# A linear recurrence beside a feed-forward layer: the first batch's preparation cut into pieces between the feed-forward steps, and three small operations moved to other engines

## The chip, the cores and the metric

The kernel runs on one core of one Trainium2 chip. The metric is the device time of one execution in microseconds (us). The engines are named as in the profile: PE is TensorE (matrix products), PEld its weight loads, DVE is VectorE, ACT is ScalarE, POOL is GpSimd, SP is SyncE, which only issues DMAs here.

## The reference, cut to what matters

The reference runs four pairs of layers over x (4 batches of 512 tokens, 512 wide); every pair adds a gated cross-attention and a gated feed-forward result to x. The change touches two of these eight parts. One is the feed-forward part of pair 0, with sign weights:

```python
hidden = jnp.einsum('bsd,hd->bsh', x, sign(up_weight)) * up_scale     # 512 -> 2048
out = jnp.einsum('bsh,dh->bsd', relu(hidden), sign(down_weight)) * down_scale
```

The other is the "cross-attention" of pair 2, which is a state-space recurrence over the context. It depends on the context alone, not on x, so the kernel may compute it early:

```python
x = jnp.einsum('ed,bld->bel', in_proj_w, ctx)             # 512 channels e, 512 positions l
xc = conv_of_4_taps(x, conv_w)                            # along l, each channel by itself
u = silu(xc + conv_b)
x_dbl = jnp.einsum('ke,bel->bkl', x_proj_w, u)            # dt_lo, B (16 rows), C (16 rows)
delta = softplus(dt_proj_w @ dt_lo + dt_proj_b)
state = state * exp(delta * A[:, n]) + (delta * u) * B[n] # for each of 16 n, along l
y = sum_n state_n * C[n] + D * u
```

The last step, the gate with silu of the layer norm of x, comes later in the kernel and is not touched.

## The kernel before, in words

The program is built with a tile framework that orders each engine's queue itself: it takes what its own estimate holds ready, by priority. Where a product on PE is "tied" to the one before it, PE's order is the order in which the program was written. All products of this stage except the transposes of the layer norm are tied.

The stage in question is `s1` (feed-forward) with the generator `states()` (recurrence) running beside it. In the profile it lies between about 646 and 1441 us. `s1` makes 64 steps: `i` counts 8 halves of batches (256 tokens each), `f2` counts 8 pairs of hidden blocks. One step issues these, in this order:

1. the chain `s_ph` on PE (16 records of 128x256, line L244),
2. `aside(1)`: one `next` of the recurrence,
3. `behind.end()`: the chain `s_acc` of the step before (8 records of 128x512, L905),
4. the two Relu evictions `s_hT` on ACT (L936),
5. `aside(1)`: one more `next` of the recurrence.

`aside` runs its `next` with a priority 4000 places later, so that the recurrence fills what the feed-forward part leaves free; PE's order is as written all the same.

The recurrence has one slot for each batch b (4), channel block e (4) and pair of n (8): 128 slots, one `yield` each. A slot first issues `summed` for the slot before, which adds two states into PSUM with eight products by the identity (`s_y`, L268), then issues two states. A state costs these: broadcast rows `s_B` and `s_C` (256 KB DMAs on SP, L1154), the product `s_db` on DVE (L1156), `s_da`, an Exp, on ACT (L1157), the scan `s_h` on DVE (L1158), and the product of `s_h` with `s_C` on POOL (L1159). `s_h` has 7 buffers, so DVE may run at most 7 states ahead of PE. When a channel block ends, `channels_done` copies the sums out of PSUM on ACT (L1190 to L1192: two half copies into `r`, one copy into `r0`), and in the next slot `rest` makes y on DVE with two operations (L1195, L1198) and writes it out.

Each batch needs its preparation first. `pieces(b)` returns nine pieces: four times `channels(e)` (product `s_pi`, copy `s_xp` on ACT, four taps on DVE at L1097 and L1099, Silu into u), then `low` (product `s_pd`), `raw(0)`, `delta((0, 1))`, `raw(2)`, `delta((2, 3))` (product `s_pv`, then Abs, Relu, Exp and Ln on ACT, with five operations on DVE for each block, L1129 to L1137). The pieces write u, delta and delta times u to DRAM rows, and the states read them back. The PSUM tile of `s_pi`, `s_pd` and `s_pv` has one buffer, so each of these products waits until ACT has read the one before.

The pieces of batches 1 to 3 are dealt one by one into every third slot of the batch before, in its channel blocks e = 0 to 2. Those of batch 0 have no batch before. They are issued in one go by `next(states)` ahead of the 64 steps, at ordinary priority, so on PE they stand ahead of the first `s_ph`.

The 64 steps make 128 `next`, just the 128 slots. The last `summed` and `channels_done` come after them. The feed-forward weights (eight tiles of 1 MB) are loaded and put through Sign on ACT (L875, L884) at the start of the stage.

Of the kernel before, what the change touches and what calls it, by code (L numbers as in the profile page):

```python
# [16 lines left out]
ALU = mybir.AluOpType  # L17
# [4 lines left out]
S = 512  # L22
# [26 lines left out]
class Net:  # L49
# [816 lines left out]


    def s1(self, states, aside):
        nc, a = self.nc, self.a
        FC = 2048 // P  # L870
        wu = []
        for c in range(DC):
            t = self.w(f"s1_wu_{c}")
            nc.sync.dma_start(t, a["s1_upT"][c * P : (c + 1) * P, :])
            nc.scalar.activation(t, t, AF.Sign)  # L875
            wu.append(t)
        wd = []
        for c in range(4):
            t = self.w(f"s1_wd_{c}")
            v = t.rearrange("p (f n) -> p f n", f=4)  # L880
            nc.sync.dma_start(
                v, a["s1_downT"][c * 512 : (c + 1) * 512, :].rearrange("(f p) n -> p f n", p=P)
            )
            nc.scalar.activation(t, t, AF.Sign)  # L884
            wd.append(v)
        us = self.s("s1_us", FC)
        nc.sync.dma_start(us, a["s1_us"].rearrange("(f p) -> p f", p=P))
        ds = self.bcast("s1_ds", a["s1_ds"])
        osc = self.s("s1_os", 1)
        nc.sync.dma_start(osc, a["s1_os"].partition_broadcast(P))  # L890
        nc.vector.tensor_scalar(ds, ds, osc, None, op0=ALU.mult)

        behind = Behind()
        xTs = {0: self.lnT("s1_0", 0)}
        next(states)
        accs = {}
        HT = TB // 2

        def down(i, f2, hT):
            if f2 == 0:  # L900
                accs[i] = [self.mm(f"s1_acc_{i}_{t}") for t in range(HT)]
            for j in range(2):
                f = 2 * f2 + j
                for t in range(HT):
                    ins = nc.tensor.matmul(  # L905
                        accs[i][t],
                        lhsT=hT[:, j, t * P : (t + 1) * P],
                        rhs=wd[f // 4][:, f % 4, :],
                        start=(f == 0),
                        stop=(f == FC - 1),  # L910
                    ).ins
                    self.tie(ins)
            if f2 == FC // 2 - 1:
                for t in range(HT):
                    r = self.t(f"s1_r_{i}_{t}")
                    nc.vector.tensor_tensor(r, accs[i][t], ds, op=ALU.mult)
                    self.residual(i * HT + t, r, self.gf[:, 0:1])

        for i in range(2 * NB):
            b, cols = i // 2, slice(i % 2 * HT * P, (i % 2 + 1) * HT * P)  # L920
            for f2 in range(FC // 2):
                if i % 2 and f2 == 0 and b + 1 < NB:
                    xTs[b + 1] = self.lnT(f"s1_{b + 1}", b + 1)
                ph = self.mm(f"s1_ph_{i}_{f2}").rearrange("p (j n) -> p j n", j=2)
                for j in range(2):
                    fs = slice((2 * f2 + j) * P, (2 * f2 + j + 1) * P)
                    self.chain(
                        ph[:, j, :], [(wu[c][:, fs], xTs[b][:, c, cols]) for c in range(DC)],
                        tied=True,
                    )  # L930
                aside(1)
                behind.end()
                hT = self.t(f"s1_hT_{i}_{f2}").rearrange("p (j n) -> p j n", j=2)
                for j in range(2):
                    f = 2 * f2 + j
                    nc.scalar.activation(  # L936
                        hT[:, j, :], ph[:, j, :], AF.Relu, scale=us[:, f : f + 1]
                    )
                behind(down, i, f2, hT, more=True)
                aside(1)  # L940
        behind.end()
# [105 lines left out]
    def states(self):  # L1047

        nc, a = self.nc, self.a
# [12 lines left out]
        cw = fixed("s4_cw", [P, EC, 4])  # L1062
# [16 lines left out]
        def pieces(b):  # L1079
            part = lambda k, e: rows[b][k][e * P : (e + 1) * P, :]  # L1080
            room = {}

            def channels(e):
                if e == 0:
                    room["cx"] = self.context("s4", b)
                    room["u"] = self.up.tile([P, EC, S], F32, tag="u4", name=f"s4_u_{b}", bufs=1)
                pi = pre(f"pi_{b}_{e}")
                self.chain(
                    pi,
                    [(wi[:, c, e * P : (e + 1) * P], room["cx"][:, c, :]) for c in range(CC)],  # L1090
                    tied=True,
                )
                xp = self.tp.tile([P, S + 3], F32, tag="t", name=f"s4_xp_{b}_{e}")
                nc.gpsimd.memset(xp[:, 0:3], 0.0)
                nc.scalar.copy(xp[:, 3 : S + 3], pi)
                xc = self.t(f"s4_xc_{b}_{e}")
                nc.vector.tensor_scalar(xc, xp[:, 0:S], cw[:, e, 0:1], None, op0=ALU.mult)  # L1097
                for k in range(1, 4):
                    nc.vector.scalar_tensor_tensor(  # L1099
                        xc, xp[:, k : S + k], cw[:, e, k : k + 1], xc, op0=ALU.mult, op1=ALU.add  # L1100
                    )
                u = room["u"][:, e, :]
                nc.scalar.activation(u, xc, AF.Silu, bias=vec[:, 0, e : e + 1])
                nc.sync.dma_start(part("u", e), u)

            def low():
                pd = pre(f"pd_{b}")[0 : 3 * N]
                self.chain(pd, [(wx[:, e, :], room["u"][:, e, :]) for e in range(EC)], tied=True)
                room["low"] = self.t(f"s4_low_{b}")
                nc.scalar.copy(room["low"][0 : 3 * N], pd)  # L1110
                nc.sync.dma_start(rows[b]["bc"], room["low"][N : 3 * N])

            def raw(e):
                pv = pre(f"pv_{b}_{e}")
                self.chain(pv, [(wdt[:, e * P : (e + 1) * P], room["low"][0:N])], tied=True)
                bias = vec[:, 1, e : e + 1]
                room["v", e], room["z", e] = (self.t(f"s4_{k}_{b}_{e}") for k in ("v", "z"))
                nc.scalar.activation(room["z", e], pv, AF.Abs, bias=bias)
                nc.scalar.activation(room["v", e], pv, AF.Relu, bias=bias)

            def delta(es):


                raw(es[1])
                vs, zs = ([room.pop((k, e)) for e in es] for k in ("v", "z"))
                z1s = [self.t(f"s4_z1_{b}_{e}") for e in es]
                for z, z1 in zip(zs, z1s):
                    nc.scalar.activation(z, z, AF.Exp, scale=-1.0)
                    nc.vector.tensor_scalar(z1, z, 1.0, None, op0=ALU.add)  # L1129
                    nc.vector.scalar_tensor_tensor(z, z1, -1.0, z, op0=ALU.add, op1=ALU.subtract)  # L1130
                for z1 in z1s:
                    nc.scalar.activation(z1, z1, AF.Ln)
                for e, v, z, z1 in zip(es, vs, zs, z1s):
                    nc.vector.tensor_tensor(z1, z1, z, op=ALU.subtract)
                    nc.vector.tensor_tensor(v, v, z1, op=ALU.add)
                    nc.sync.dma_start(part("dl", e), v)
                    nc.vector.tensor_tensor(z1, v, room["u"][:, e, :], op=ALU.mult)  # L1137
                    nc.sync.dma_start(part("du", e), z1)

            return (  # L1140
                [lambda e=e: channels(e) for e in range(EC)]
                + [low]
                + [lambda: raw(0), lambda: delta((0, 1)), lambda: raw(2), lambda: delta((2, 3))]
            )

# [30 lines left out]
        yield  # L1176
        for piece in pieces(0):
            piece()
        yield
        def row(k, b, e):  # L1180
            t = self.qp.tile(
                [P, S], F32, tag=f"r{k}", name=f"s4_r{k}_{b}_{e}", bufs=1 + (k != "u")
# [4 lines left out]
        def channels_done(b, e, u, y):  # L1187

            r, r0 = self.t(f"s4_yr_{b}_{e}"), self.t(f"s4_y0_{b}_{e}")
            nc.scalar.copy(r[0:64], y[64:128, 1, :])  # L1190
            nc.scalar.copy(r[64:128], y[0:64, 1, :])
            nc.scalar.copy(r0, y[:, 0, :])  # L1192

            def rest():
                nc.vector.scalar_tensor_tensor(  # L1195
                    u, u, vec[:, 2, e : e + 1], r0, op0=ALU.mult, op1=ALU.add
                )
                nc.vector.tensor_tensor(u, u, r, op=ALU.add)  # L1198
                nc.sync.dma_start(rows[b]["y"][e * P : (e + 1) * P, :], u)

            return rest
# [984 lines left out]
```

## Time and profile before

| | us |
|---|---|
| median of 3 runs | 3196.8 (3187.31 to 3198.38) |
| the profiled execution | 3203.01 |
| its span | 3201.1 |
| PE busy in the span | 2821.5 (88%) |
| DVE busy in the span | 1952.0 (61%) |
| ACT busy | 1196.0 (37%) |
| POOL busy | 975.8 (30%) |
| the stage: its first product (`s_pi`) starts, the first product of the next stage (`s_pkv`) starts | 646.62 to 1440.69 |
| first and last scan of the stage | 695.48, 1427.41 |

The shares are means over eight parts with different limits, so the stage must be read by itself. The page's line engine operation groups give a busy total, a mean in ns of one instruction, and the idle time of the engine before it. A view by windows gives busy time by stretch. A timeline row gives start, duration, engine, line, operation and count.

### The profile page before, as it was taken

The numbers are of one execution on the slowest core, as the hardware profiler recorded it, in microseconds if no ns is written. First come the engines' busy times: TensorE is split into PE (matmuls) and PEld (weight loads), VectorE is DVE, ScalarE is ACT, GpSimd is POOL, SyncE is SP. The second block draws the span as 40 slices with busy tenths as digits, with TensorE's granted clock in tenths as the row PEclk, the third lists the DMA queues.
The fourth block names the chain that finished last, engine by engine and source line by source line (L and its number), as shares of the span: only waits on it lengthen the run. The fifth ranks groups of instructions, "written<-read, shape, count | busy, mean of one in ns | idle before, by whom it ended". The sixth has DMA issues, their size and how long they took to land.

```text
span 3201.1 us, 43082 instructions
## 1 busy us (share of the span) xinstructions
PE 2821.5 (88%) x15776; PEld 1442.0 (45%) x15776; DVE 1952.0 (61%) x3212; ACT 1196.0 (37%) x2061; POOL 975.8 (30%) x939
## 2 busy tenths in 40 slices
PE   6899898768988989997786699977999999989999
PEld 2333333234444444443344588862333333345774
DVE  6565666378897979987788311118666666735004
ACT  2343443365554445433222111112554545521331
POOL 3465654516555655760000122210000000001440
PEclk8899999879999989999897699997999999989999
DMA  4000000177676767862212599973000000013996
GB/s 133 7 1 7 1 1 1 20 252 238 195 229 176 236 206 224 250 196 84 77 64 90 176 320 326 322 259 137 14 29 14 29 1 1 1 53 122 379 384 225
DMA packets 266897, 438.75 MB, mean 137 GB/s; under 512 B 32400, under 2 KB 114576, under 8 KB 265152
## 3 DMA queue, kind: packets, MB, share of 16 engines
q1 hardware_dynamic: 250624, 386.72, 37.8%
q0 software_dynamic: 13760, 45.10, 3.9%
q10 hardware_dynamic: 2304, 4.20, 0.3%
q8 instruction: 126, 2.06, 0.3%
q14 instruction: 83, 0.68, 0.1%
HBM read 370.79 MB, written 65.13 MB: 136 GB/s over the span
## 4 chain that ended last, share of the span: by engine, by line
PE 60%; DVE 16%; POOL 9%; ACT 6%; issue 6%; DMA 3%; SPq 0%; DVEq 0%; POOLq 0%; ACTq 0%
PE s_pl L268 12%; PE s_po L244 11%; PE pg_s L244 7%; PE s_ph L244 6%; POOL s_h L1159 6%; PE s_pq L244 4%; PE s_av L268 3%; ACT pr_s L1957 2%; PE s_pb L244 2%; DVE s_h L1158 2%; PE s_acc L905 2%; PE s_pkv L244 1%; PE pt_s L223 1%; DVE x L863 1%; POOL es_s L746 1%
## 5 line engine op out<-in xcount | busy, mean ns | idle before, releaser
L1159 POOL TENSOR_TENSOR s_h<-s_h,s_C 128x512 f32<-128x512 f32 x256 | 448.1, 1751 | 290.3 <-DVE s_h L1158 248.6
L268 PE MATMUL s_pl<-s_qT,s_kT 32*128 32x512 f32 (+1 forms) x1536 | 447.3, 658 | 60.4 <-ACT pr_s L846 23.5
L268 PE MATMUL s_ps<-s_kT,s_qT 32*128 32x512 f32 (+1 forms) x1536 | 441.1, 677 | 12.7 <-DVE s_top L1837 5.9
L1837 DVE TENSOR_REDUCE s_top<-s_ps 128x1 f32<-128x512 f32 x512 | 328.5, 685 | 108.7 <-PE s_ps L268 108.6
L1957 ACT ACTIVATE pr_s<-s_pl 128x512 f32<-128x512 f32 x512 | 277.9, 595 | 307.4 <-PE s_ps L268 297.7
L1158 DVE TENSOR_TENSOR_SCAN s_h<-s_da,s_db 128x512 f32<-128x512 f32 x256 | 312.1, 1219 | 62.5 <-PE s_y L268 36.1
L1157 ACT ACTIVATE s_da<-s_rdl,s_A 128x512 f32<-128x512 f32 x256 | 184.4, 722 | 329.2 <-DVE s_h L1158 328.4
L1331 POOL MEMSET s_room<- 128x128 f32 (+1 forms) x2 | 0.5, 258 | 998.9 <-PE s_av L268 678.8
L268 PE MATMUL s_av<-pr_s,s_v 128*32 128x256 f32 (+1 forms) x3072 | 250.9, 398 | 0.2
L244 PE MATMUL s_ph<-xT_s,s_wu 128*128 128x256 f32 x1024 | 247.9, 397 | 0.7 <-ACT xT_s L161 0.7
L905 PE MATMUL s_acc<-s_wd,s_hT 128*128 128x512 f32 x512 | 239.9, 612 | 5.7 <-ACT s_hT L936 5.7
L244 PEld LDWEIGHTS s_ph<-xT_s,s_wu 128*128 128x128 f32 x1024 | 198.2, 198 | 78.8 <-issue 50.2
L244 PEld LDWEIGHTS pg_s<-s_xbT,s_w 128*128 128x128 f32 (+1 forms) x1872 | 214.7, 184 | 19.8 <-issue 17.8
L268 PEld LDWEIGHTS s_pl<-s_qT,s_kT 32*128 32x128 f32 (+1 forms) x1536 | 118.4, 186 | 227.1 <-ACT pr_s L1957 95.8
L244 PE MATMUL pg_s<-s_xbT,s_w 128*128 128x128 f32 (+1 forms) x1872 | 216.2, 276 | 1.4 <-ACT s_xbT L161 1.4
L694 DVE TENSOR_REDUCE s_nmx<-s_ps 128x1 f32<-128x496 f32 x256 | 158.4, 662 | 91.6 <-PE s_ps L268 81.3
L1156 DVE TENSOR_TENSOR s_db<-s_B,s_rdu 128x512 f32<-128x512 f32 x256 | 203.8, 796 | 10.7 <-DMA s_B<-s_bc 2.8
L846 ACT ACTIVATE pr_s<-s_pl 128x512 f32<-128x512 f32 (+1 forms) x256 | 138.7, 593 | 158.9 <-PE s_pl L268 82.9
L268 PE MATMUL s_y<-s_h,ident 64*64 64x512 f32 x1024 | 147.6, 640 | 49.5 <-issue 32.3
L268 PEld LDWEIGHTS s_av<-pr_s,s_v 128*32 128x32 f32 (+1 forms) x3072 | 61.4, 109 | 286.0 <-issue 253.9
L1552 DVE TENSOR_TENSOR g_s<-g_s,pg_s 128x256 f32<-128x256 f32 x78 | 27.5, 352 | 264.5 <-ACT g_s L1551 264.5
L1446 POOL DMA_INDIRECT s_xb<-s_xs,s_from x86 | 83.2, 968 | 333.0 <-PE ptr_s_xb L234 176.1
(388 smaller groups left out, 4460.4 us busy)
## 6 DMA issues: line engine op xcount, KB each, us to landing
s_B<-s_bc SPq DMA_DIRECT2D x256, 256.0 KB
s_C<-s_bc SPq DMA_DIRECT2D x256, 256.0 KB
s_w<-in_s_wg SPq DMA_DIRECT2D x39, 704.0 KB
s_w<-in_s_wu SPq DMA_DIRECT2D x39, 704.0 KB
s_w_rt<-in_s_ru SPq DMA_DIRECT2D x47, 512.0 KB
s_w_rt<-in_s_rd SPq DMA_DIRECT2D x47, 512.0 KB
s_w<-in_s_wd SPq DMA_DIRECT2D x39, 512.0 KB
s_y<-s_ys SPq DMA_DIRECT2D x32, 512.0 KB
```

Source lines behind the costliest of these rows:

```text
L244: ins = self.nc.tensor.matmul(out, lhsT=l, rhs=r, start=(i == 0), stop=(i == len(pairs) - 1)).ins
L268: ins = self.nc.tensor.matmul(out, lhsT=l, rhs=r, **flags).ins
L694: ins = nc.vector.tensor_reduce(nmx[:, at + i : at + i + 1], ps[i][0][:, 0:M], axis=AX.X, op=ALU.max, negate=True,).ins
L846: ins = nc.scalar.activation(prs[i][0:n, j, :], pl[j][0][0:n, :], AF.Exp).ins
L905: ins = nc.tensor.matmul(accs[i][t], lhsT=hT[:, j, t * P : (t + 1) * P], rhs=wd[f // 4][:, f % 4, :], start=(f == 0), stop=(f == FC - 1),).ins
L1156: nc.vector.tensor_tensor(db, br, du, op=ALU.mult)
L1157: nc.scalar.activation(da, dl, AF.Exp, scale=am[:, e, n : n + 1])
L1158: nc.vector.tensor_tensor_scan(h, da, db, 0.0, op0=ALU.mult, op1=ALU.add)
L1159: nc.gpsimd.tensor_tensor(h, h, cr, op=ALU.mult)
L1446: self.nc.gpsimd.indirect_dma_start(out=t, out_offset=None, in_=self.sorted[name][1], in_offset=bass.IndirectOffsetOnAxis(ap=fr[:, j : j + ...
L1837: ins = nc.vector.tensor_reduce(dst[:, i], ps[i][0], axis=AX.X, op=ALU.max, negate=True).ins
L1957: ins = nc.scalar.activation(prs[i][:, j, :], pl[j][0], AF.Exp).ins
```

## The change

It has three parts.

Batch 0's preparation. The `next(states)` ahead of the 64 steps is gone. In `states()` each of the nine pieces of batch 0 is now followed by a `yield`, and three empty `yield`s follow them, so the first 12 `next` of the steps carry the pieces and nothing, and the slots begin with the 13th. To have enough of them, every fifth step makes two in its first `aside`. With 13 such steps there are 141 `next`: nine pieces, three empty ones, 128 slots and the tail. The pieces of batch 0 so come at the lower priority of `aside`, and their products stand on PE between the `s_ph` and `s_acc` of steps 0 to 3.

Operations to ScalarE. The first tap of the convolution and the sum 1 + z, for each of the 16 channel blocks of the four batches, go from DVE to ACT.

One addition to GpSimd. The two halves of y are added on POOL right after the copies; DVE's second operation in `rest` is gone.

```diff
         behind = Behind()
         xTs = {0: self.lnT("s1_0", 0)}
-        next(states)
         accs = {}
...
-                aside(1)
+
+                aside(2 if (i * FC // 2 + f2) % 5 == 2 else 1)
                 behind.end()
...
                 xc = self.t(f"s4_xc_{b}_{e}")
-                nc.vector.tensor_scalar(xc, xp[:, 0:S], cw[:, e, 0:1], None, op0=ALU.mult)
+                nc.scalar.mul(xc, xp[:, 0:S], cw[:, e, 0:1])
...
                     nc.scalar.activation(z, z, AF.Exp, scale=-1.0)
-                    nc.vector.tensor_scalar(z1, z, 1.0, None, op0=ALU.add)
+                    nc.scalar.add(z1, z, 1.0)
...
         for piece in pieces(0):
             piece()
-        yield
+            yield
+
+        for _ in range(3):
+            yield
+
...
             nc.scalar.copy(r0, y[:, 0, :])
+            nc.gpsimd.tensor_tensor(r, r, r0, op=ALU.add)
 
             def rest():
                 nc.vector.scalar_tensor_tensor(
-                    u, u, vec[:, 2, e : e + 1], r0, op0=ALU.mult, op1=ALU.add
-                )
-                nc.vector.tensor_tensor(u, u, r, op=ALU.add)
+                    u, u, vec[:, 2, e : e + 1], r, op0=ALU.mult, op1=ALU.add
+                )
                 nc.sync.dma_start(rows[b]["y"][e * P : (e + 1) * P, :], u)
```

## The prediction

> **What bounds the kernel now.** I read the page for the engines, then the stage by windows, then the waits of DVE, then single rows. All that the change touches lies between 646 and 1441 us, so the other seven parts are taken as unmoved. The windows cut the stage at the first scan, at the first scan of batches 1, 2 and 3, and at the last scan's end:
>
> ```profile
> core 0: us, PE busy (x) PEld busy (x) DVE busy (x) ACT busy (x) POOL busy (x), PEclk, DMA share, GB/s
> 646.00:686.00 40.00, 23.99 (x50) 7.75 (x48) 25.14 (x46) 32.56 (x35) 0.58 (x3) 0.76 0.72 258
> 686.00:695.50 9.50, 6.02 (x17) 4.38 (x16) 4.93 (x9) 7.11 (x11) 0.10 (x1) 0.77 0.65 223
> 695.50:884.00 188.50, 165.71 (x641) 82.62 (x642) 165.32 (x188) 98.54 (x146) 112.60 (x67) 0.91 0.72 217
> ...
> 1274.80:1428.60 153.80, 147.25 (x633) 75.60 (x626) 140.80 (x143) 63.06 (x106) 111.11 (x64) 1.00 0.79 234
> 1428.60:1440.70 12.10, 12.10 (x50) 4.79 (x48) 1.77 (x4) 0.84 (x2) 3.19 (x7) 1.00 0.26 88
> ```
>
> For 40 us PE has only preparation and is busy for 24 of them, at a granted clock of 0.76. Then, from the first scan (695.5) to the last one's end (1428.6), PE and DVE are both close to full: two engines share the bound. DVE's waits in those 733.1 us:
>
> ```profile
> DVE s_h L1158 <- PE s_y L268: 36.1, 16, 6.3
> DVE s_xc L1097 <- ACT s_xp L1095: 5.3, 9, 0.6
> DVE xT_s L162 <- PE pt_s L223: 4.1, 5, 1.3
> ```
>
> They come to some 50 us, of which 36 are scans that find all seven `s_h` full because PE is behind. What one step and one state cost undisturbed:
>
> ```profile
> 1386.81 1.09 PE L268 MATMUL s_y<-s_h,ident 64*64 64x512 f32 x8
> 1387.83 3.72 PE L244 MATMUL s_ph<-xT_s,s_wu 128*128 128x256 f32 x16
> 1391.48 1.09 PE L268 MATMUL s_y<-s_h,ident 64*64 64x512 f32 x8
> 1392.50 3.70 PE L905 MATMUL s_acc<-s_wd,s_hT 128*128 128x512 f32 x8
> 1396.13 1.09 PE L268 MATMUL s_y<-s_h,ident 64*64 64x512 f32 x8
> ...
> 1425.32 1.22 DVE L1158 TENSOR_TENSOR_SCAN s_h<-s_da,s_db 128x512 f32<-128x512 f32 x1
> ...
> 1427.41 1.22 DVE L1158 TENSOR_TENSOR_SCAN s_h<-s_da,s_db 128x512 f32<-128x512 f32 x1
> ```
>
> By their starts, PE needs 3.65 + 3.63 + 2 x 1.02 = 9.32 us for a step with two slots, 4.66 a slot. DVE needs 2.09 us a state, 4.18 a slot, and has the pieces, the layer norms, the residuals and y besides. So PE leads where no pieces run (batch 3), DVE where they do.
>
> **Part 1: batch 0's pieces move into the steps.** Removed is the stretch in which PE waits for the chain of pieces. The first `s_ph` needs only the four Sign results of `s_wu`; the first of these starts at 651.77 in the trace, and four at 1.91 us without pieces between them end at 659.4. That is 27 us earlier than the first `s_ph` of now (686.3). But the first scan gets later, because feed-forward products stand between the pieces:
>
> - `s_ph` 0 at 659.4, 5.7 us as the first one takes now: 665.1. `s_pi` 0 (1.9): 667.0. Its copy (0.57), `s_pi` 1: 669.6. `s_ph` 1 (3.65): 673.3. `s_pi` 2, `s_acc` 0, `s_pi` 3: 680.7. `s_ph` 2 ends at 684.4.
> - `low` needs the last u: copy 0.57, first tap on ACT 0.6, three taps 2.33, table load 1.28, Silu 0.72, so 686.2; `s_pd` (3.6) ends at 689.8.
> - copy 0.58, `s_pv`, `s_acc` 1, `s_pv` 1: 696.2; Abs and Relu 1.35; Exp 0.63; 1 + z 0.6; table load 1.28; two Ln 1.26; then two DVE operations of 0.69 for the first block, beside the second Ln: the first write of delta at about 702.2.
> - now the first write of delta is issued at 682.12 and the first scan starts at 695.48, 13.4 us later; kept, that gives a first scan at 715.5, 20 us later than now.
>
> Every DMA of the pieces moves along: u, bc, dl and du writes and the reads back, in SP's order. They are counted in the 13.4 us; SP is otherwise held by waits for POOL (354 us of them on L1154), which cost nothing while scans aren't waiting for rows (2.8 us in all). The context load stands before the weights in SP's queue now. If it falls behind them, it still lands before 665: the 258 GB/s of the first window bring the 8 MB by then. The Sign of `s_wd` (7.6 us) runs on ACT beside `s_ph` 0 and ends by 667.0.
>
> In return some 5.5 steps of feed-forward, 5.5 x 7.28 = 40 us of PE, are done before the scans. The rest carries 11 slots in five steps: (5 x 7.28 + 11 x 1.02) / 11 = 4.33 us of PE a slot instead of 4.66, 42 us over 128 slots. PE then falls under DVE nearly everywhere, so DVE's waits for PE go. Not all: about three times 5 us lie at the layer norms, where PE waits for DVE's own work and the scans then wait for PE. I take 20 of the 36.1 us as gone (bounds 8 and 34).
>
> **Parts 2 and 3: what DVE is spared while scanning** (batches 1 to 3 have 12 blocks of pieces):
>
> ```profile
> L1129 DVE TENSOR_SCALAR s_z<-s_z 128x512 f32<-128x512 f32 x12 | 10.4, 865 | 0.0
> L1198 DVE TENSOR_TENSOR s_ru<-s_ru,s_yr 128x512 f32<-128x512 f32 x15 | 10.2, 681 | 0.2
> L1097 DVE TENSOR_SCALAR s_xc<-s_xp,s_cw 128x512 f32<-128x512 f32 x12 | 8.7, 727 | 5.3 <-ACT s_xp L1095 5.3
> ```
>
> The first tap: 8.7 us and 5.3 of idle go if DVE's order changes so that a scan fills the time of ACT's copy and product. If the order stays, the second tap waits for an ACT instruction of about 0.6 us (the copy L1095 takes 0.57) and 12 x 0.6 = 7.2 come back. Between 1.5 and 14 I take 9, since the framework orders by readiness. 1 + z the same: 10.4, less 7.2 at worst; I take 7. ACT pays 2 x 12 x 0.6 = 14 us in this stretch, hidden by 328 us in which `s_da` waits for the scan before (ACT's waits; ACT is busy for 353 of the 733 us); with that cover gone, `s_da` and behind it the scans would be late by as much. No table is loaded at the lines that copy or scale now, so I add none.
>
> The addition of the halves: DVE loses 10.9 us (16 x 0.68), POOL gains 16 x 1.27 (its product L1159 alone takes 1.27; with DVE in the way 1.77). It stands in POOL's queue among the products with `s_C`. What a POOL instruction does to DVE is in these rows:
>
> ```profile
> 712.47 1.69 POOL L1159 TENSOR_TENSOR s_h<-s_h,s_C 128x512 f32<-128x512 f32 x1 [2.42 <-DVE s_h L1158]
> ...
> 712.96 1.76 DVE L1156 TENSOR_TENSOR s_db<-s_B,s_rdu 128x512 f32<-128x512 f32 x1
> ...
> 716.54 0.70 DVE L1156 TENSOR_TENSOR s_db<-s_B,s_rdu 128x512 f32<-128x512 f32 x1
> 716.59 1.77 POOL L1159 TENSOR_TENSOR s_h<-s_h,s_C 128x512 f32<-128x512 f32 x1 [2.38 <-DVE s_h L1158]
> ```
>
> Started first, POOL makes `s_db` 1.76 us long instead of 0.70. The Trainium skill speaks against this move: "Perfetto Trace Analysis", section "Optimizing Scalar/DVE Operations", says that the two engines share a read port that a DVE operation with two SBUF inputs holds exclusively, so that shifting work between them might not help; by it the whole hold counts, 16 x 1.27 = 20.3 less 10.9, a loss of 9. In the steady rhythm POOL is free 2.09 - 1.77 = 0.32 us between its products, so an addition of 1.27 started there runs about 0.9 us into `s_db`: 16 x 0.9 = 14.4 less 10.9, a loss of 4. If it falls into the 2.5 us in which POOL now idles around y, it is a gain of 10.9. I take the loss of 4, as the rows show the collision.
>
> **The sum.** The scans take 733.1 - 20 - (9 + 7 - 4) = 701 us, from 715.5 to 1416.5. At the end PE is no longer behind: one POOL product, `s_y` and the last `s_acc`, 1.3 + 1.1 + 3.7 and waits, 7 us instead of 12.1. The stage ends at 1423.5 instead of 1440.7: 17 us less. The profiled execution, 3203.0 (span 3201.1), lies 6.2 above the median; 17 off the median 3196.8 is 3180. About 0.5%, 16 us, is what a measurement of this kernel can tell from no change.
>
> **The rivals.**
>
> *The gap at the start is the whole gain* (0.14). If the pieces' chain overlaps better (first scan at 706, the reads no longer beside 8 MB of weights), PE's lag vanishes (34 of 36) and the taps are filled in (14 + 10 - 4): 706 + 733.1 - 54 + 7 = 1392, 48 us less, 3149. For it: DVE's bound alone is lower still. Against: the layer norms.
>
> *Late start, no faster scans* (0.10). First scan at 722, since the eight general tiles `t` of this pool must hold `s_hT` beside nine temporaries of a piece; only 8 us of lag and 5 of DVE go: 722 + 720 + 7 = 1449, 8 slower, 3205.
>
> *POOL's queue becomes the bound* (0.18; slower). The addition waits for three ACT copies, and these for the last `s_y` of a block; behind it on POOL stand the next products, and PE's `s_y` waits for those. Today only DVE's y operation waits so, and DVE shows almost none of it (0.9 us). If the queue is ordered a slot too early, each of 16 blocks loses about a slot of lead, 4.66 less POOL's slack of about 2: 16 x 2.5 = 40 us, 23 slower, 3220. It decides from 17 / 16 = 1.1 us a block. Against: the framework placed the y operation well.
>
> *The change does not reorder* (in the first case's lower end): the pieces' products keep PE waiting just where it waited; the sum loses the 20 us, 3200.
>
> **How the numbers follow.** The likeliest case (0.58) has 3180, with 3160 to 3200 of its own: 0.35 of it lies over 16 us faster, 0.23 within. With 0.14 from the first rival, faster is 0.49; with 0.08 of the second rival, same is 0.31; with 0.18 and 0.02, slower is 0.20. The range, 3145 to 3215, takes in the first rival and half of the slower one.
>
> **What would show it.** Right: first `s_ph` near 660, first scan near 715, batch 0's products between feed-forward chains, last scan near 1416, DVE's wait for `s_y` under 20 us, `s_acc` last. The page would show DVE without L1198's group, and ACT up by some 19 us (32 x 0.6). Wrong: a first scan beyond 725; POOL rows waiting for ACT's copies by more than 1 us each; `s_db` with more than 40 long rows of 1.76; or a scanning stretch above 720 us.

## The result, and the profile after: 0.35% slower

| | before | after |
|---|---|---|
| median of 13 runs, us | 3196.8 (3187.31 to 3203.81) | 3209.08 (3198.46 to 3211.03) |
| ratio to before (95% interval) | | 1.0035 (1.0024 to 1.0046) |
| profiled execution, its span | 3203.01, 3201.1 | 3201.37, 3199.5 |
| first `s_ph`, from the end of the stage before | 39.5 | 7.6 |
| first scan | 48.7 | 61.7 |
| first scan to the end of the last one | 733.1 | 723.7 |
| from there to PE's last product of the stage | 12.1 | 13.0 |
| the stage | 794.0 | 798.4 |

The forecast was 17 us faster; the median is 12 us slower. The profiled execution of after hides it: its span is shorter than before's only because the stage ahead ended at 641.9 us instead of 646.8. So all marks here count from that end, the last `s_po`, and the stage ends with PE's last product of it. The changed kernel was profiled a second time (`all_again` below): 61.7, 727.2, 13.0, and 801.9 for the stage. One profile's stage is thus good to some 4 us, and the loss that the two profiles place in the stage is 4 to 8 of the 12 us. Where the rest lies stays open. One later stretch, from the first `s_pq` to the first `pg_s`, took between 361 and 368 us from one profile to another; in before and in both profiles of after it took about 367.

The next stage's first product, `s_pkv`, which bounded the stage in the account of before, starts at 793.9 in before but at 804.4 and 808.0 in after:

```profile
1446.25 2.04 PE L244 MATMUL s_pkv<-s_wkv,ctx_s 128*128 128x512 f32 x2 [5.96 <-DMA s_wkv<-in_s_wkv]
```

PE stands there for the weights `s_wkv`. SP issued their load at 1441.08, right behind the last write of y; in before it was issued at 1429.18, ahead of that write. Every kernel with part 1 has such a gap, of 4 to 6 us. Little of it is lost: the product behind, `s_pq`, starts only 5.2 and 8.9 us later than in before, where PE stood 3.4 us for that one.

The stage after by windows: the Signs, up to the first scan, the stretch up to batch 1, batch 3 and the tail.

```profile
core 0: us, PE busy (x) PEld busy (x) DVE busy (x) ACT busy (x) POOL busy (x), PEclk, DMA share, GB/s
641.90:649.50 7.60, 3.38 (x17) 2.74 (x17) 7.25 (x16) 2.99 (x5) 0.20 (x2) 0.67 1.01 402
649.50:703.60 54.10, 50.16 (x143) 27.03 (x144) 17.34 (x28) 42.52 (x57) 0.32 (x1) 0.92 0.53 178
703.60:888.40 184.80, 165.64 (x659) 82.92 (x657) 162.28 (x186) 100.86 (x154) 115.49 (x71) 0.94 0.69 219
...
1270.00:1428.00 158.00, 144.16 (x603) 72.91 (x602) 133.34 (x139) 62.38 (x104) 116.88 (x69) 0.95 0.76 227
1428.00:1446.20 18.20, 12.29 (x46) 5.57 (x44) 6.08 (x13) 4.06 (x7) 4.29 (x11) 0.92 0.26 87
```

The start is as meant: PE is busy for 50 of the 54 us ahead of the first scan, at a granted clock of 0.92 instead of 0.76. But once the scans run it is hardly fuller than before: 165.6 of 184.8 us, where before had 165.7 of 188.5, and 144 of 158 in batch 3, where before had 147 of 154. What DVE waited for between the first scan and the last:

```profile
DVE s_ru L1200 <- POOL s_yr L1197: 27.2, 12, 2.6
DVE s_h L1158 <- PE s_y L268: 24.7, 22, 5.9
DVE s_xc L1099 <- ACT s_xc L1097: 12.1, 9, 1.3
DVE s_z L1134 <- ACT s_z L1132: 5.1, 6, 1.3
```

Before had 36.1, 5.3 and none other above 4.1. The wait for PE fell by 11 us and two new ones came, for POOL's addition (27.2 us, at 12 of the 15 ends of channel blocks in this stretch) and for ACT's first tap (12.1, where before had 5.3 for ACT's copy).

### The profile page after: what moved, and what is told of

The parts are those of the page before. It is cut to its first block, busy times and chain, and to the rows that moved or that the text cites. A ratio compares the mean times of both kernels' runs of the same rounds, so it can differ in the third digit from the quotient of the medians.

```text
span 3199.5 us, 42966 instructions
## 1 busy us (share of the span) xinstructions
PE 2817.9 (88%) x15776; PEld 1441.8 (45%) x15776; DVE 1915.9 (60%) x3164; ACT 1210.5 (38%) x2090; POOL 994.3 (31%) x955
## 4 chain that ended last, share of the span: by engine, by line
PE 45%; DVE 8%; ACT 3%; POOL 2%; DMA 1%; issue 1%; SPq 0%; POOLq 0%; DVEq 0%; ACTq 0%
PE s_po L244 9%; PE s_pl L268 8%; PE pg_s L244 7%; PE s_ph L244 5%; ACT pr_s L1961 2%; PE s_pb L244 2%; PE s_pq L244 2%; PE s_av L268 2%; POOL s_h L1159 2%; DVE x L863 1%; PE s_acc L904 1%; PE pt_s L223 1%; PE ptr_s_xb L234 1%; PE s_pr L244 1%; PE s_y L268 1%
## 5 line engine op out<-in xcount | busy, mean ns | idle before, releaser
L1158 DVE TENSOR_TENSOR_SCAN s_h<-s_da,s_db 128x512 f32<-128x512 f32 x256 | 312.1, 1219 | 52.8 <-PE s_y L268 24.7
L904 PE MATMUL s_acc<-s_wd,s_hT 128*128 128x512 f32 x512 | 246.4, 626 | 4.3 <-ACT s_hT L936 4.3
L1156 DVE TENSOR_TENSOR s_db<-s_B,s_rdu 128x512 f32<-128x512 f32 x256 | 191.3, 747 | 9.4 <-DMA s_B<-s_bc 0.7
## 6 DMA issues: line engine op xcount, KB each, us to landing
s_w_rt<-in_s_rd SPq DMA_DIRECT2D x47, 512.0 KB, 12.9
```

The lines of the kernel that those rows point to most:

```text
L904: ins = nc.tensor.matmul(accs[i][t], lhsT=hT[:, j, t * P : (t + 1) * P], rhs=wd[f // 4][:, f % 4, :], start=(f == 0), stop=(f == FC - 1),).ins
L1156: nc.vector.tensor_tensor(db, br, du, op=ALU.mult)
L1158: nc.vector.tensor_tensor_scan(h, da, db, 0.0, op0=ALU.mult, op1=ALU.add)
```

## The experiments

The first expectations name four theories: POOL's addition eats the gain (A), the 12 us lie outside the stage (B), the denser slots cost it (C), ACT's waits are the loss (D). Behind them stand two readings of DVE's wait for `s_y`. *PE's work:* it comes from how much PE has to do; the move cures it, and another part takes the gain back. *A hand-over:* it comes from a point that no part of the change touches; this one was put to the test later. In the tables "scans" means from the first scan's start to the last one's end, in one profile.

### One part at a time

`all_again` is the changed kernel itself, `move_only` part 1 of the change (batch 0's preparation), `act_only` part 2, `pool_only` part 3, and `no_pool` parts 1 and 2. Their diffs are the corresponding hunks of the change.

> The changed kernel once more, for a second profile of it. Theory A (the addition on GpSimd eats the gain): the stage from 646 to 1446 us looks as in the first profile, first scan near 703, last near 1427, VectorE waiting some 40 us for the added row on GpSimd, and the ratio is again about 1.0035. Theory B (the 12 us of the medians lie outside the stage, in later stages that get another timing): the span is 6 to 10 us longer than in the first profile while the stage's marks are within 3 us of it.

> Part 1 alone on the kernel before: batch 0's pieces between the steps, all operations on their old engines. Theory A: first feed-forward product near 650, first scan near 703, and without the waits for GpSimd and ScalarE the last scan comes 15 to 25 us earlier than the 1428.6 of before, so 10 to 20 us faster than before. Theory C (the denser slots themselves cost it, since the layer norm falls on a block that has pieces): the scans take 724 us or more, and the time is that of before or up to 12 us slower.

> Part 2 alone on the kernel before: first tap and 1 + z on ScalarE. Theory A: VectorE waits for these some 40 us in place of the 19 us that it is spared, in part while TensorE leads anyway: within 6 us of before, rather slower. Theory D (ScalarE's waits are the main loss): 10 us or more slower.

> Part 3 alone on the kernel before: the halves of y added on GpSimd. Theory A: each of 16 y operations on VectorE waits some 2.4 us for GpSimd in place of the 0.6 us saved, 15 to 30 us slower than before. Theory C or D: within 5 us of before.

> The changed kernel without part 3: both y operations back on VectorE. If the added row on GpSimd is what costs the changed kernel against the move alone, the scans take 722 us or less and the time is that of the move alone, 3198 (ratio about 1.0005). If the parts' costs only add up, the scans take some 724 us, a ratio near 1.002. If part 2 is the loss, it stays at 1.0035.

| | ratio (95%) | first scan | scans | stage |
|---|---|---|---|---|
| before | 1 | 48.7 | 733.1 | 794.0 |
| `all_again` | 1.0035 (1.0021 to 1.0048) | 61.7 | 727.2 | 801.9 |
| `move_only` | 1.0008 (1.0000 to 1.0015) | 59.7 | 722.7 | 795.2 |
| `act_only` | 0.9997 (0.9988 to 1.0006) | 52.4 | 734.4 | 799.4 |
| `pool_only` | 1.0006 (0.9998 to 1.0014) | 48.7 | 735.9 | 797.2 |
| `no_pool` | 1.0017 (1.0007 to 1.0026) | 61.7 | 720.6 | 795.2 |

No part gains. (`act_only`'s longer stage does not show in its time: the later stretch spoken of above took 360.7 us in its profile and 367.6 in before's.) The scans' changes add: -10.4 + 1.3 + 2.8 = -6.3, 726.8, where the whole change has 723.7 and 727.2. Theory A was wrong on both of its numbers: the move alone was to be 10 to 20 us faster, part 3 alone 15 to 30 slower, and both are within 3 us of before. B wanted the stage's marks unmoved within 3 us from one profile to the other, and the scans of `all_again` are 3.5 us longer than in the first. C had the time of the move alone right and its scans (724 us or more) just wrong. `act_only`'s time does not bear out D. Part 1 pays for 10.4 us of shorter scans with a first scan 11.0 later. Its wait of DVE for `s_y`, which the theory of PE's work puts under 20 us, and PE's work in the scanning stretch, in before and in `move_only`:

```profile
DVE s_h L1158 <- PE s_y L268: 33.7, 30, 5.8
```

```profile
695.50:1428.60 733.10, 664.72 (x2641) 334.96 (x2642) 646.67 (x703) 353.01 (x546) 447.31 (x266) 0.94 0.73 219
707.30:1430.00 722.70, 641.66 (x2550) 319.69 (x2549) 640.13 (x708) 350.31 (x541) 449.59 (x267) 0.92 0.73 221
```

33.7 instead of 36.1. PE has 23 us less to do in the scanning stretch, and DVE waits for it nearly as before. That theory does not hold. Most of the 10.4 us are DVE's own instructions: the 255 `s_db` fell from 203.1 to 195.4 us.

By batches, the move takes 3.2, 5.8 and 4.9 us off the first three and adds 3.6 to the last (157.4 for 153.8), the one in which the prediction had PE leading. There PE's granted clock was 0.92 instead of 1.00, and its idle time right behind the copies spoken of below 13.4 us instead of 6.6. No run tells these two apart.

Part 2 alone. DVE's waits, then its groups of line and operation (busy us, mean ns, idle before), and, below, the same two groups in before:

```profile
DVE s_h L1158 <- PE s_y L268: 43.6, 24, 6.4
DVE s_xc L1099 <- ACT s_xc L1097: 12.1, 9, 1.3
...
DVE s_z L1134 <- ACT s_z L1132: 2.6, 5, 1.0
```

```profile
L1130 DVE SCALAR_TENSOR_TENSOR s_z<-s_z,s_z 128x512 f32<-128x512 f32 x12 | 14.2, 1219 | 0.0
L1099 DVE SCALAR_TENSOR_TENSOR s_xc<-s_xp,s_cw,s_xc 128x512 f32<-128x512 f32 x36 | 30.0, 834 | 12.8 <-ACT s_xc L1097 12.1
```

```profile
L1130 DVE SCALAR_TENSOR_TENSOR s_z<-s_z,s_z 128x512 f32<-128x512 f32 x12 | 8.2, 681 | 0.2
L1099 DVE SCALAR_TENSOR_TENSOR s_xc<-s_xp,s_cw,s_xc 128x512 f32<-128x512 f32 x36 | 27.0, 750 | 1.1
```

The two groups that left DVE had 19.1 us. But the operations that follow them grew, L1130 by 6.0 us and L1099 by 3.0. So, with smaller changes both ways elsewhere, all of DVE's durations fell by only 15. Against that stand three waits: 6.8 more for ACT's first tap (12.1 for 5.3), 2.6 for `s_z`, and 7.5 more for `s_y`. Together +1.9; the scans grew by 1.3. The saving is there and is all waited away. On top of the move, part 2 takes 2.1 us off the scans and starts them 2.0 later (`no_pool` beside `move_only`).

Part 3 alone. DVE's waits:

```profile
DVE s_h L1158 <- PE s_y L268: 31.7, 13, 6.4
DVE s_ru L1196 <- POOL s_yr L1193: 19.2, 8, 2.4
```

The collision that the forecast priced did not get worse: `s_db` has 13 rows of 1.4 us or more, before has 22. The loss has another form. DVE reaches its y operation before POOL has made the sum, and mostly stands still 2.4 us. (Three more such waits stand under other labels.) In the whole change, at the end of one block:

```profile
1406.28 1.26 POOL L1197 TENSOR_TENSOR s_yr<-s_yr,s_y 128x512 f32<-128x512 f32 x1
...
1407.57 0.75 DVE L1200 SCALAR_TENSOR_TENSOR s_ru<-s_ru,s_vec,s_yr 128x512 f32<-128x512 f32 x1 [2.38 <-POOL s_yr L1197]
```

Before, DVE spent 21.3 us (L1195, mean 1419 ns) and 10.2 (L1198) there; after, 11.2 us (L1200, mean 749) and 27.2 of waits: 38.4 for 31.5.

### Less work on DVE, less on PE, an earlier norm

These three, on top of `move_only`, ask which engine's amount of work the scans are short of. `dve_spared` leaves out the weight of the first tap and takes 1 + z into Ln's bias, with nothing given to ACT. `pe_spared` leaves out the second chain of the eight steps with `f2 == 3`, so an eighth of the down projection, 29 us of PE. `norm_ahead` applies the layer norm of the next batch two steps before its transposes.

```diff
-                nc.vector.tensor_scalar(xc, xp[:, 0:S], cw[:, e, 0:1], None, op0=ALU.mult)
...
-                    nc.vector.tensor_scalar(z1, z, 1.0, None, op0=ALU.add)
...
+                    nc.scalar.activation(z, z, AF.Ln, bias=self.ones[:, 0:1])
```

```diff
-            for j in range(2):
+            for j in range(2 if f2 != 3 else 0):
```

```diff
                 if i % 2 and f2 == 0 and b + 1 < NB:
-                    xTs[b + 1] = self.lnT(f"s1_{b + 1}", b + 1)
+                    xl = self.ln(f"s1_{b + 1}", self.x[(b + 1) * TB : (b + 2) * TB])
+                if i % 2 and f2 == 2 and b + 1 < NB:
+                    xTs[b + 1] = self.lnT(f"s1_{b + 1}", b + 1, xl=xl)
```

> On the move alone: the first tap is left out (its weight taken as one) and the sum 1 + z is folded into the bias of the Ln, so VectorE loses what part 2 takes from it and ScalarE gets nothing for it. It leaves out the first tap's weight. If VectorE bounds the scans as the prediction held, they get 16 to 25 us shorter than the 722.7 of the move alone. If TensorE and VectorE wait for each other in turn and VectorE's spare time goes into waits for TensorE, they get less than 8 us shorter.

> On the move alone: eight of the 64 steps leave out their second product chain (eight matmuls each, 8 x 3.63 = 29 us of TensorE). It leaves out an eighth of the down projection. If VectorE bounds the scans, under 8 us are gained; if TensorE does, 20 to 29; if the two are coupled, something between, 8 to 20.

> On the move alone: the layer norm of the next batch is applied two steps ahead of its transposes instead of right before them. In the move alone TensorE stands some 10 us at each of three transposes until VectorE has made the norm, and the scans then stand until TensorE has caught up. If these three places are the coupling, the scans get 15 to 30 us shorter and the time falls to some 3175 to 3185. If VectorE's own work for the norm (some 8 us each) is what counts, it stays within 5 us of the move alone.

| | ratio (95%) | scans | stage |
|---|---|---|---|
| `dve_spared` | 0.9996 (0.9984 to 1.0009) | 717.8 | 791.3 |
| `pe_spared` | 1.0002 (0.9991 to 1.0013) | 718.4 | 791.1 |
| `norm_ahead` | 0.9991 (0.9982 to 1.0000) | 718.6 | 791.2 |

Each takes only 4 to 5 us off `move_only`'s 722.7, each less than its main theory asked for. The first lets two groups of DVE operations go, which lowers DVE's durations by 12.9 us in all, the second 29 us of products on PE. So the amount of work on neither engine, by itself, is what holds the scans. Two things follow. Taking part 2's operations away, with no new wait for ACT's results, was worth 4.9 us on the move; giving them to ACT gained 2.1. And the lower clock of `move_only` in the scanning stretch (0.92 instead of 0.94, in the lines by windows above) explains little: by an estimate it is some 14 us of PE's 642, and 28 us of PE were worth 4.3 here.

### The hand-over of the sums

What does is seen at the ends of the channel blocks. One of them in before, PE's rows of the timeline and then ACT's:

```profile
848.58 1.09 PE L268 MATMUL s_y<-s_h,ident 64*64 64x512 f32 x8
849.60 3.70 PE L905 MATMUL s_acc<-s_wd,s_hT 128*128 128x512 f32 x8
858.00 1.98 PE L268 MATMUL s_y<-s_h,ident 64*64 64x512 f32 x8 [4.70 <-issue]
```

```profile
854.40 0.63 ACT L1132 ACTIVATE s_z<-s_z 128x512 f32<-128x512 f32 x1 [0.65 <-DVE s_z L1130]
855.47 0.63 ACT L1132 ACTIVATE s_z<-s_z 128x512 f32<-128x512 f32 x1 [0.43 <-DVE s_z L1130]
856.12 0.58 ACT L1190 COPY s_yr<-s_y 64x512 f32<-64x512 f32 x1
856.72 0.58 ACT L1191 COPY s_yr<-s_y 64x512 f32<-64x512 f32 x1
857.32 0.58 ACT L1192 COPY s_y<-s_y 128x512 f32<-128x512 f32 x1
```

The block's last `s_y` is done by 849.7. The copies that take its sums out of PSUM run only from 856.12, because ACT's queue holds a piece of delta ahead of them, whose two Ln wait for DVE. The next `s_y` starts 0.1 us after the third copy: the PSUM tile `y` has one buffer. PE stood 4.7 us, which the row labels "issue". Summed over 15 such ends, the idle time of PE that ends right behind a third copy is 41.3 us in before. In `move_only` it is 48.1, at 13 ends; one of them:

```profile
1288.69 0.58 ACT L1194 COPY s_yr<-s_y 64x512 f32<-64x512 f32 x1
1289.28 0.58 ACT L1195 COPY s_yr<-s_y 64x512 f32<-64x512 f32 x1
1289.89 0.59 ACT L1196 COPY s_y<-s_y 128x512 f32<-128x512 f32 x1
```

```profile
1290.57 1.99 PE L268 MATMUL s_y<-s_h,ident 64*64 64x512 f32 x8 [4.64 <-POOL s_h L1159]
```

The same 0.1 us behind the copy, under another label: an `s_y` waits for two things, and the view names one. The test takes the dependence away and keeps the work: the three copies read u instead of the sums, so y is no longer the reference's. `sums_free` does so in before, `sums_free_move` with part 1, `sums_free_act` with part 2.

```diff
-            nc.scalar.copy(r[0:64], y[64:128, 1, :])
-            nc.scalar.copy(r[64:128], y[0:64, 1, :])
-            nc.scalar.copy(r0, y[:, 0, :])
+            nc.scalar.copy(r[0:64], u[64:128])
+            nc.scalar.copy(r[64:128], u[0:64])
+            nc.scalar.copy(r0, u)
```

> On the kernel before: ScalarE's three copies at the end of a channel block read the row u from SBUF in place of the sums in PSUM, so the sums are never read and y is left wrong; counts and sizes stay. The PSUM tile of the sums has one buffer, so now TensorE's first sum of a block waits until ScalarE, in its queue's order, has copied the last block. If this hand-over at 15 block ends is where TensorE and VectorE lose their time, TensorE's 32 us of waits without a shown releaser go and the scans get 15 to 35 us shorter than 733. If the lookahead of seven states is too short everywhere, under 8 us.

> The same on the move alone. If the hand-over is what kept the move's gain from showing, the scans fall from 722.7 to some 685 to 700, the stage ends 20 to 35 us earlier, and the difference between this kernel and the same on the kernel before is near the 17 us of the prediction. If not, the scans stay above 714.

> Part 2 on the kernel before with the copies reading u in place of the sums (y is left wrong). With the hand-over gone, VectorE waits for TensorE only 9 us and is the bound. If the hand-over hid part 2's gain, the scans get 10 to 16 us shorter than the 707.8 of the same kernel without part 2. If the waits for ScalarE take the gain, they stay within 5 us of it.

| | ratio (95%) | first scan | scans | stage |
|---|---|---|---|---|
| `sums_free` | 0.9899 (0.9884 to 0.9915) | 48.7 | 707.8 | 765.9 |
| `sums_free_move` | 0.9917 (0.9904 to 0.9931) | 59.0 | 699.9 | 766.9 |
| `sums_free_act` | 0.9937 (0.9921 to 0.9953) | 52.3 | 707.5 | 771.1 |

This decides between the theories. Without the hand-over both kernels lose 28 us of their stage. DVE's wait for `s_y` in `sums_free`, and PE's largest there:

```profile
DVE s_h L1158 <- PE s_y L268: 9.3, 3, 3.4
```

```profile
PE pt_s L223 <- DVE xl_s L205: 24.6, 3, 8.5
```

So 27 of the 36.1 us are the hand-over, which the change does not touch. The three waits left each come some 10 to 13 us behind one of the three places where PE stands for DVE's layer norm; a steady lag of PE is not among them. The move gains 7.9 us of scans here and starts 10.3 later, so it only trades; the 17 us that its expectation gave it without the hand-over did not come. Part 2 gains 0.3 of scans here and starts 3.6 later, so the hand-over was not what hid its gain. In `sums_free_act` DVE's durations fall by 7.7 us, and its waits for ACT grow by 10.6: 13.4 us for the first tap (`sums_free`: 5.7 at this place) and 2.9 for `s_z`. What the same operations would give here if nothing had to wait for ACT was not run.

### Can the order repair it, or more room?

`copies_first` (on `move_only`) ties the first Exp of the next block behind the last copy. `handover` does so on before, and ties y's first DVE operation behind the scan. `handover_ln` adds Ln with 1 as its bias and drops the correction of the rounding of 1 + z, three DVE operations less a block. `handover_move` adds part 1 to `handover`. `h_eight` gives `move_only` an eighth `s_h` buffer.

```diff
-            nc.scalar.activation(da, dl, AF.Exp, scale=am[:, e, n : n + 1])
+            ins = nc.scalar.activation(da, dl, AF.Exp, scale=am[:, e, n : n + 1]).ins
+            if copied:
+                self.tc.add_manual_dep(ins, copied.pop().name, ...)
...
-            nc.scalar.copy(r0, y[:, 0, :])
+            copied.append(nc.scalar.copy(r0, y[:, 0, :]).ins)
```

```diff
-                for k, bufs in (("B", 4), ("C", 5), ("da", 2), ("h", 7))
+                for k, bufs in (("B", 4), ("C", 5), ("da", 2), ("h", 8))
```

> On the move alone, with the result kept: ScalarE's order is tied so that the three copies of the sums stand ahead of the Exp of the next slot's first state. If the hand-over waits in ScalarE's queue behind such Exps, TensorE's waits at block ends shrink from some 4 us to under 2 and the scans get 8 to 25 us shorter. If VectorE's lookahead over the block end is worth as much, nothing is gained or up to 15 us are lost.

> On the kernel before, with the result kept: ScalarE's three copies of the sums tied ahead of the Exp of the next slot's first state, and VectorE's first y operation tied behind the scan of the slot that it is issued in, so that VectorE doesn't stand waiting for the copies, as it did for 34 us in copies_first. If the hand-over in the queues' order is the cause, 8 to 30 us faster than before. If lookahead lost at the block end costs as much as the wait, within 5 us.

> The kernel handover, and 1 + z taken out of VectorE by the bias of the Ln; with it go the operation that corrects its rounding and the subtraction of that correction, so three operations of each of the 16 blocks, some 2 us, with nothing put on ScalarE. If VectorE now bounds the scans, 10 to 22 us faster than handover; else under 6.

> The kernel handover with batch 0's pieces moved between the steps (part 1). If VectorE bounds the scans once the hand-over is repaired, the move only delays the first scan by 11 us and saves less: 0 to 8 us slower than handover. If it is TensorE, 5 to 15 us faster.

> On the move alone: eight buffers for the states in place of seven. If VectorE's waits for TensorE come from too short a lookahead, the 33 us of waits shrink by 5 to 15 and the scans with them. If they come from single places at which TensorE itself stands for long, under 4 us.

| | ratio (95%) | scans | stage |
|---|---|---|---|
| `copies_first` | 1.0021 (1.0013 to 1.0030) | 731.6 | 799.4 |
| `handover` | 1.0077 (1.0061 to 1.0093) | 758.3 | 812.5 |
| `handover_ln` | 0.9991 (0.9984 to 0.9999) | 740.4 | 792.0 |
| `handover_move` | 1.0055 (1.0038 to 1.0071) | 736.9 | 804.7 |
| `h_eight` | 0.9989 (0.9981 to 0.9997) | 716.5 | 791.1 |

The order repairs nothing, and `handover` was slower by more than its expectation allowed for: it only names another engine as the one that waits. DVE's waits in `copies_first`, then in `handover`:

```profile
DVE s_ru L1207 <- ACT s_y L1204: 34.0, 10, 9.1
...
DVE s_h L1166 <- PE s_y L268: 0.6, 2, 0.5
```

```profile
DVE s_h L1166 <- ACT s_da L1159: 56.1, 15, 8.3
```

In `copies_first` DVE's wait for PE goes from 33.7 to 0.6 us, and a wait of 34.0 for the copies takes its place. In `handover` the scans wait 56.1 us for the Exp that is held behind the copies. In each order that was tried, someone waits at the end of a block for the one PSUM tile to be emptied. No run gave `y` a second buffer, so whether that would end it is not shown. An eighth `s_h` buffer lets DVE run one state further and gives 6.2 us of scans. `handover_ln` differs from `handover` in the three operations alone: DVE's durations fall by 34 us and the scans by 17.9. `handover_move` has scans 21.4 us shorter than `handover`, more than was expected of the move; no run says why.

### A version that beats both

`lighter` is before with Ln's bias and without the correction, so with delta rounded a little otherwise, and with eight `s_h` buffers. `lighter_move` adds part 1 and the earlier layer norm.

```diff
-                    nc.vector.tensor_scalar(z1, z, 1.0, None, op0=ALU.add)
-                    nc.vector.scalar_tensor_tensor(z, z1, -1.0, z, op0=ALU.add, op1=ALU.subtract)
-                for z1 in z1s:
-                    nc.scalar.activation(z1, z1, AF.Ln)
+                for z, z1 in zip(zs, z1s):
+                    nc.scalar.activation(z1, z, AF.Ln, bias=self.ones[:, 0:1])
...
-                    nc.vector.tensor_tensor(z1, z1, z, op=ALU.subtract)
```

> On the kernel before, batch 0's pieces in front: 1 + z folded into the bias of the Ln, without the correction of its rounding (three VectorE operations less in each of 16 blocks), and eight buffers for the states. In the kernels with the hand-over tied this saved 20 us; here part of it goes into waits for TensorE at block ends: 8 to 22 us faster than before.

> The same with part 1, and the layer norm applied two steps ahead of its transposes, which gained 4 us of scans on the move alone: 10 to 28 us faster than before. If the move only trades, within 6 us of lighter; if part 1 is good once VectorE is lighter, 8 or more ahead of lighter.

`lighter` has 3178.57 us, 0.9943 (0.9928 to 0.9958); scans 715.2, stage 777.6. `lighter_move` has 3179.56, 0.9936 (0.9917 to 0.9954); 695.9 and 772.3, with the first scan 14 later. Both came as expected. How much of the 17.9 us of scans that `lighter` gains is the eighth buffer's and how much the three operations' was not run apart; on the move the buffer gave 6.2. Here too the move brings no gain that the times can tell.

## Why the prediction was wrong, point by point

- **The start: right, and better than forecast.** The first `s_ph` came 31.9 us earlier (forecast 27), the first scan 13.0 later (forecast 20). PE's products of batch 0 stand between the feed-forward chains as said.
- **"I take 20 of the 36.1 us as gone": the first step that failed.** `move_only`'s scans are 10.4 us shorter, but its wait for `s_y` is 33.7: 2.4 of it went, less than the lower bound of 8. The prediction read this wait as PE being behind with its work, 4.66 us a slot against 4.18. `sums_free` shows that 27 of it are the hand-over of the sums, and that the 9.3 left lie behind the layer norms, where the prediction had left some 15. The work taken out was over-sized too: 5.5 steps, 40 us, were to be done ahead of the scans, and `move_only` has five chains of `s_ph` and three and a half of `s_acc` there, where before had one of `s_ph`. That is 23 us of PE's busy time. The signs were in the rows of before: a wait of 36.1 us in only 16 events, six of which hold 29.9, is not a steady lag of half a microsecond a slot, and PE had 32.3 us of "issue" at `s_y` in the same stretch:

```profile
PE s_y L268 <- issue: 32.3, 11, 6.8
PE s_y L268 <- POOL s_h L1159: 17.2, 6, 6.4
```

- **"I take 9 ... I take 7": the second, and the largest.** Part 2 was to give 16 us and gave -1.3 (`act_only`), 0.3 without the hand-over. The worst case had been reckoned as 12 x 0.6 us of new waits for each of the two, 14.4. They came to 9.4, so that price was sound and the choice near its good end was not: DVE waited for ACT instead of filling the time. And two items had no place in the working: of the 19.1 us that left DVE its durations kept 4, since the operations behind the removed ones grew, and the waits at `s_y` grew by 7.5. The working took every microsecond taken off DVE as one off the scans; `dve_spared`, with no wait for ACT, turned 12.9 into 4.9.
- **"I take the loss of 4": right in size (2.8 alone; 3.1 to 6.6 on top of the other two), wrong in its form.** It is not a longer `s_db`, by the shared port or otherwise; it is DVE standing for POOL's sum, 27.2 us in the whole change, less 20.3 of DVE time saved at y. That the size came out near 4 is luck. The slower rival named this place, but put 2.5 us a block on it and on PE; the wait is 1.8 a block over 15, on DVE, and 0.5 of it is lost when the saving is taken off.
- **The tail: 13.0, forecast 7.** After the last scan PE is busy for 12.3 us (the last window), as before for 12.1: part of the feed-forward chains is still to be done there, so the work taken out at the start did not end it sooner. The later start of `s_pkv` behind it had no place in the forecast.
- **A slip that cost nothing.** 8 MB at 258 GB/s take 32 us, some 4 more than there are from the weights' first issue (636.3) to 665. But the context load kept its place ahead of them (630.4 in after).
- **The sum.** Scans forecast 701, measured 723.7 and 727.2: 9.6 from the move, 17.3 from part 2, less 1.2 from part 3, is 25.7 of it. Beside this, 7 better at the start and 6 worse at the end: 22 to 25 us worse in all than the forecast of 17 less, which is the 4 to 8 us that the stage is longer.

By its own list of signs: the first `s_ph`, the place of batch 0's products, `s_acc` as the last product and, roughly, ACT's busy time (up by 14.5 us instead of 19) say right; the scanning stretch above 720 us and DVE's wait for `s_y` over 20 (24.7) say wrong. Two signs of being wrong stayed away: `s_db` has 11 long rows, not 40, and POOL waited over 1 us at no more than three of the 16 ends. DVE waiting for POOL was on neither list.

## What to carry to other kernels

When an engine waits often and long at a few places and hardly between them, look for the one tile that is handed over there before counting work: find the instruction that ends just before the idle time does, whatever label the view gives. Before you move an operation off a full engine, price the wait for its result at the place where that engine needs it: part 2's waits for ACT took 9.4 of the 15 us that DVE was spared. And do not count even a removed operation as a whole gain: where two engines wait for each other, `dve_spared` turned 12.9 us of DVE into 4.9 of scans, and `handover_ln` 34 into 17.9. Work moved ahead of a recurrence delays its start, and here that took back what it shortened.

## What was not expected of the hardware

A DVE operation that is removed does not always give its time back. In before the sum 1 + z took 865 ns on DVE in the mean and the operation after it, L1130, 681; in `act_only`, with the sum on ACT, L1130 takes 1219. Of the 10.4 us that left, 6.0 came back in L1130, which reads two inputs from SBUF. The rows of `act_only` show how:

```profile
1018.75 1.77 POOL L1159 TENSOR_TENSOR s_h<-s_h,s_C 128x512 f32<-128x512 f32 x1 [1.99 <-DVE s_h L1158]
1019.32 1.76 DVE L1130 SCALAR_TENSOR_TENSOR s_z<-s_z,s_z 128x512 f32<-128x512 f32 x1
...
1021.00 0.68 DVE L1130 SCALAR_TENSOR_TENSOR s_z<-s_z,s_z 128x512 f32<-128x512 f32 x1
```

Six of the twelve L1130 take 1.76 us; each begins 0.6 us after a POOL product has begun and ends about 0.55 behind that product's end. The other six take 0.68. In before it is the sum that falls on a POOL product, at five of twelve places, and takes 1.49 instead of 0.42, while L1130 stays under 0.7 each time. So the delay that the sum had taken passed to the next operation. This is in line with the read port that DVE and POOL share by the Trainium skill ("Perfetto Trace Analysis", "Optimizing Scalar/DVE Operations"). POOL's addition took 1.26 us at most of the places where DVE stood still for it, and 1.4 in the mean.
